# Two transformer layers on one core: the output bias of attention in four tiles, a count moved, the last routing amid expert tiles, other banks at a stage's exit, the last rows in two stores

## The chip, the core and the metric

The kernel runs on one core of one Trainium2 chip. A core has engines with a queue of instructions each: TensorE (PE in the profile; PEld its weight loads), VectorE (DVE), ScalarE (ACT), GpSimd (POOL) and SyncE (SP), which here only issues DMAs. [...] They wait for each other through semaphores. Matmuls write into PSUM[...]; everything else is in SBUF or in DRAM. The metric is the device time of one execution in microseconds.

## The reference

Eight sequences of 512 rows and 512 columns pass through two layers. All weights and activations are float32.

```python
# layer 0
x = layernorm(x + attn0(x))     # causal, 16 heads of 32; q, k, v and output with a bias
#   attn0: out = softmax(mask(q k^T / sqrt(32))) v ;  return out @ WO.T + WO_b
x = layernorm(x + moe(x))       # router: softmax over 8 experts, the two largest, weights renormalised
#   expert: (silu(gate) * up) @ down, with low-rank additions; y = sum of the two experts by weight
# layer 1
x = layernorm(x + attn1(x))     # norm, 8 query heads on 2 key heads of 64, no mask, own residual
x = layernorm(x + ffn(x))       # hidden 1408, weights integers minus 128 by a scale per row
```

The kernel sends each row only to its two experts, by a table of rows that it builds on the way.

## The kernel before, in words

**Attention of layer 0** (`attention0`, lines 1298 to 1653). The loop goes over sequences b = 0..7, groups of four heads g = 0..3 and units u = 0..2 of the causal score matrix (UNITS, key tiles 0; 1 and 3; 2). A unit is: scores on TensorE (L65), the exponential on ScalarE (L1476), one or two `affine_select` on POOL that zero what lies above the diagonal (L1486; two in unit 1), and one unit later the product with v (L1503) and VectorE's sums of p (L1511). At unit 1 the group before is normalised: row sums rs (L1518), their reciprocal (L1521) and the product into aoT (L1522). Between these stand pieces of other work that `plan(b)` hands out: q, k and v of the groups to come, the output projection of sequence b-1 (`project`, L1402, with layernorm, L190 to L198, and stores into `rows`), and its routing. For sequences 0 to 5 the normalised rows are turned through DRAM: 32x32 blocks on VectorE (L98), four stores and one load (L103, L106), then the router's logits (`score`, L504) at unit 2 of group 3. Sequence 6 is turned on TensorE (L1427), sequence 7 after the heads. `choose` finds the two experts (L523 to L554), `dispatch` the ranks (L568 to L578), `one_hot` (L591, L592) and `enter` (L601 to L603) put rows into the table.

**The order.** TensorE's order is the order in which the program is written (`in_order`). VectorE, ScalarE, POOL and SP in attention 0 get theirs from a planner at build time: by its own costs it sees what is ready, and takes the earliest in the program of that. From the expert stage (step 12) to the end of attention 1 all are in program order; in the feed-forward part the planner orders again, up to the last rows.

**Buffers that the change meets.** The pool "mm" has two PSUM banks; each `mm(...)` takes the one that was taken the time before last, and waits until it has been read. Scores have one buffer of four banks. SBUF tiles with the same tag share a buffer: `first_turned` (tag "row", L1575 on) takes that of `row`, which holds the bias of v and the output bias; `first_rows` takes that of a sequence's x. `first_turned` receives, at unit 1 of group 3 of sequence 7, the first expert rows turned (L924, copied by ScalarE at L925).

**The output bias** is added to x by one POOL instruction for a sequence, at group 2 (L1595). In the trace the planner has put it where x has just landed, in group 3 of the sequence before (for sequences 2 to 7).

**The first expert tiles** (`Tiles`) begin amid the end of attention 0. They use rows of sequences 0 to 5 only, after a count that says whether four tiles of each of the first four experts are full (`soon`, L613 to L615). A `step` on TensorE is one half of the hidden layer for a pair of tiles (`half`, 16 matmuls, L958) and one `down` (4 matmuls, L983); it also fetches rows (POOL, L873) and turns them. The routing of sequence 7 stands between steps 3 to 6.

**Exit of attention 1** (`batches`, from L1955). The last projections use four banks; residuals (L1804), statistics and norms (L1823) follow on VectorE. `IntegerFfn.run` then opens its PSUM pools, `p_gu` first. **End**: `last_rows` normalises a tile of 128 rows at a time; the last on VectorE (L1288), then one store by ScalarE's queue (L1293).

## Time and profile before

| what | value |
|---|---|
| median of 3 runs | 2107.35 us (2106.85 to 2108.73) |
| profiled execution | 2106.08 us |
| its span, first to last instruction | 2104.2 us |
| attention 0, to about 690 us | TensorE busy 677.4 us |
| routing amid tiles, 690 to 770 us | TensorE busy 78.1 of 80 us |
| expert tiles, 770 to 1062 us | TensorE busy 291.5 of 292 us |
| attention 1, 1062 to 1600 us | TensorE busy 535.9 of 538 us |
| feed-forward, 1600 to the end | TensorE busy 491.6 us |

The times are those of one profiled execution, which differs from the median by 1.3 us. In a row of the time line the first number is the start in us from the span's start, the second the length; "xN" is how many instructions of one kind were merged; the bracket at the end tells how long the engine was idle before and which instruction ended that ("<-"). In a row of waits the three numbers are the sum in us, the count and the longest.

### The profile page before, as it was taken

The page shows a single profiled execution, that of the slowest core. Times are in us where ns is not written, and L with a number is a line of the kernel's source. Part 1 is how long each engine was busy: PE and PEld are TensorE (multiplying, and loading weights), DVE is VectorE, ACT ScalarE, POOL GpSimd, SP SyncE. Part 2 cuts the span into 40 slices and gives each one's busy share as a digit, 9 for nine tenths or more (in the row PEclk, how much of TensorE's full clock was granted, in tenths as well). Part 3 has the DMA queues.
Part 4 walks back from the last instruction along what each step waited for, and adds up shares of the span by engine and source line. Part 5 has one row for each costly group of instructions (what it writes and reads, how often), then busy time and mean ns, then how long its engine had stood idle before and what let it go on. Part 6 is the DMA issues. An engine that isn't in the chain of part 4 may idle for free. (4 is left out here: it accounts for less than half of the span.)

```text
span 2104.2 us, 35813 instructions
## 1 busy us (share of the span) xinstructions
PE 2074.4 (99%) x15074; PEld 1048.8 (50%) x15074; DVE 1270.6 (60%) x1963; ACT 606.8 (29%) x840; POOL 496.0 (24%) x488
## 2 busy tenths in 40 slices
PE   8999999999999999999999999999999999999998
PEld 2333333333334677774433333333335888888886
DVE  2666776776768623234257898887867644555443
ACT  2333433324333111111143333333332322222222
POOL 2343534434333221222042221223101000000000
PEclk9999999999999999999999999999999999999999
DMA  9020303415222568877451322132102311111000
GB/s 326 22 65 38 101 22 110 136 52 156 85 98 102 172 199 239 251 227 209 149 206 51 100 81 71 56 95 81 41 1 71 100 41 61 60 61 60 21 21 22
DMA packets 181946, 213.39 MB, mean 101 GB/s; under 512 B 72570, under 2 KB 125818, under 8 KB 178706
## 3 DMA queue, kind: packets, MB, share of 16 engines
q1 hardware_dynamic: 170496, 175.34, 26.8%
q0 software_dynamic: 10560, 34.61, 5.6%
q8 instruction: 121, 1.98, 0.4%
q10 hardware_dynamic: 722, 1.07, 0.1%
q14 instruction: 47, 0.39, 0.1%
HBM read 132.58 MB, written 78.40 MB: 100 GB/s over the span
## 5 line engine op out<-in xcount | busy, mean ns | idle before, releaser
L1077 POOL TENSOR_TENSOR g_total<-g_total,r_inv 128x512 f32<-128x512 f32 x64 | 90.1, 1408 | 488.3 <-DVE r_inv L1862 269.9
L1476 ACT ACTIVATE p<-sc 128x2048 f32<-128x2048 f32 (+1 forms) x96 | 153.0, 1594 | 174.7 <-PE sc L65 150.7
L1511 DVE TENSOR_TENSOR p<-p 128x1536 f32<-128x1536 f32 (+2 forms) x96 | 149.5, 1557 | 77.6 <-POOL p L1486 74.4
L1227 DVE SCALAR_TENSOR_TENSOR hT<-ps_u,vec,sg 128x512 f32<-128x512 f32 x88 | 65.6, 745 | 187.2 <-PE ps_u L1222 187.1
L1238 PE MATMUL ps_f<-ffn_w,h_half 128*128 128x512 f32 x664 | 168.1, 393 | 2.6 <-DVE h_half L1233 2.0
L958 PE MATMUL ps_gu<-xrT,experts 128*128 128x256 f32 x736 | 166.7, 380 | 0.4 <-DMA xrT<-pair 0.4
L958 PEld LDWEIGHTS ps_gu<-xrT,experts 128*128 128x128 f32 x736 | 139.5, 190 | 35.6 <-issue 19.2
L1832 ACT ACTIVATE p<-sc 128x1024 f32<-128x1024 f32 x128 | 124.2, 1022 | 100.2 <-PE sc L65 91.5
L1862 DVE RECIPROCAL r_inv<-r_inv 128x512 f32<-128x512 f32 x32 | 107.1, 3346 | 67.8 <-ACT r_inv L1074 67.8
L1238 PEld LDWEIGHTS ps_f<-ffn_w,h_half 128*128 128x128 f32 x664 | 122.9, 188 | 34.6 <-DVE h_half L1233 8.0
L1222 PE MATMUL ps_g<-x_high,ffn_w 128*128 128x512 f32 x352 | 137.3, 390 | 0.9 <-DVE x L1804 0.9
L1222 PE MATMUL ps_g<-x_low,ffn_w 128*128 128x512 f32 x352 | 137.2, 390 | 0.0
L1222 PE MATMUL ps_u<-x_low,ffn_w 128*128 128x512 f32 x352 | 137.1, 390 | 0.0
L1222 PE MATMUL ps_u<-x_high,ffn_w 128*128 128x512 f32 x352 | 137.1, 389 | 0.0
L65 PE MATMUL sc<-qT,kT 64*64 64x512 f32 x1024 | 124.7, 602 | 1.2 <-ACT qT L1729 0.9
L65 PE MATMUL ps_q<-experts 128*32 128x512 f32 x1024 | 120.8, 601 | 4.9 <-DMA experts<-in_xT 4.6
L65 PE MATMUL ps_v<-experts 128*32 128x512 f32 x1024 | 120.9, 595 | 0.0
L1851 PE MATMUL av<-p,v 128*64 128x512 f32 x512 | 120.9, 594 | 0.0
L1486 POOL TENSOR_SCALAR_AFFINE_SELECT p<-p 128x512 f32<-128x512 f32 x128 | 82.7, 657 | 157.6 <-ACT p L1476 155.0
L1225 ACT ACTIVATE sg<-ps_g,vec 128x512 f32<-128x512 f32 x88 | 60.6, 689 | 199.8 <-PE ps_g L1222 199.8
L65 PE MATMUL ps_o<-attn_out,aoT 128*64 128x512 f32 x512 | 116.4, 598 | 0.0
L65 PE MATMUL ps_k<-experts 128*32 128x512 f32 x1024 | 116.3, 595 | 0.0
(278 smaller groups left out, 3248.3 us busy)
## 6 DMA issues: line engine op xcount, KB each, us to landing
results<-y SPq DMA_DIRECT2D x68, 256.0 KB, 3.2
pair<-xrT SPq DMA_DIRECT2D x30, 512.0 KB, 3.0
xrT<-pair SPq DMA_DIRECT2D x120, 128.0 KB, 3.8
turned<-turned SPq DMA_DIRECT2D x56, 256.0 KB, 4.0
x<-in_x SPq DMA_DIRECT2D x8, 1024.0 KB, 8.6
rows<-x SPq DMA_DIRECT2D x32, 256.0 KB, 2.3
x<-rows SPq DMA_DIRECT2D x16, 512.0 KB, 12.5
experts<-in_xT SPq DMA_DIRECT2D x7, 1024.0 KB, 8.5
```

The source lines that it names most:

```text
L65: nc.tensor.matmul(out[m], lhsT=lhsT[:, m], rhs=rhs, start=start, stop=stop)
L958: nc.tensor.matmul(ps[:, j, :], lhsT=w, rhs=xT[:, c, :], start=c == 0, stop=c == ND - 1)
L1077: self.nc.gpsimd.tensor_tensor(self.total, self.total, r_inv, ALU.add)
L1222: nc.tensor.matmul(ps, lhsT=w[:, ts(dc, P)], rhs=x[:, dc, :], start=(dc, i) == (0, 0), stop=(dc, i) == (ND - 1, 1))
L1227: nc.vector.scalar_tensor_tensor(hT, u, vec[:, V_SU + c : V_SU + c + 1], sg, ALU.mult, ALU.mult)
L1238: self.nc.tensor.matmul(os[t], lhsT=h[:, ts(t, P)], rhs=self.weights(2 * NHID + c), start=(c, i) == (0, 0), stop=(c, i) == (NHID - 1, 1))
L1476: nc.scalar.activation(p, sc[:, :, :width], AF.Exp, scale=scale)
L1486: nc.gpsimd.affine_select(out=first, in_=first, pattern=[[0, 4], [1, P]], compare_op=ALU.is_ge, fill=0.0, base=0, channel_multiplier=-1)
L1511: nc.vector.tensor_tensor(total[:, :, P * kt :], total[:, :, P * kt :], p[:, :, at : at + w], ALU.add)
L1832: nc.scalar.activation(p, sc, AF.Exp, scale=scale)
L1851: nc.tensor.matmul(st["av"][HD * j : HD * (j + 1), :], lhsT=st["v"][:, kt, HD * j : HD * (j + 1)], rhs=p[:, j, :], start=kt == 0, stop=kt ...
L1862: nc.vector.reciprocal(r_inv, r_inv)
```

## The change

1. **Output bias.** For sequences 1 to 7 the bias is added in four POOL instructions of 128x512, tile g at unit 1 of group g, each ordered behind the last select of that unit. For sequence 0 it stays one instruction, at unit 1 of group 2.
2. **Count and table.** `soon` no longer counts on TensorE; it copies four columns of the running count. The count is taken later, in `tables`, beside the one that is there. In sequence 7 the read of the table's bank is ordered ahead of the product into aoT of the group before (`behind`). A small tile (`lane`) moves into a buffer that exists.
3. **Routing of sequence 7.** `choose` and `dispatch` go inside steps 4 and 5, between the half and the down, instead of ahead of steps 4 and 5; the one_hots go ahead of steps 6 and 7, and `enter` behind step 7.
4. **Exit of attention 1.** The pool `p_o` is opened ahead of `p_gu`, so they exchange banks, and the projections take the second bank of a scores buffer instead of the first.
5. **Last rows.** The last tile is normalised in two halves of 256 columns, each stored by its own DMA, on SP's and on ScalarE's queue.

```diff
@@ Router.enter, soon, tables
-        nc.vector.tensor_tensor(self.table, ps, self.table, ALU.add)
+        read = nc.vector.tensor_tensor(self.table, ps, self.table, ALU.add)
         nc.vector.tensor_tensor(self.table, held, self.table, ALU.add)
+        return read
...
-    def soon(self, pool, ps, held):
+    def soon(self, pool):
         nc, half = self.nc, E // 2
-        nc.tensor.matmul(ps, lhsT=self.ones, rhs=self.carry, start=True, stop=True)
-        nc.vector.tensor_reduce(held, ps[:, :half], AX.X, ALU.min)
-        nc.vector.tensor_scalar(held, held, float(SOON * P), None, ALU.is_ge)
+        self.soon_carry = pool.tile([P, half], F32, name="r_soon_carry")
+        nc.vector.tensor_copy(self.soon_carry, self.carry[:, :half])
...
+        half = E // 2
+        ps, soon = ps[:, :E], ps[:, E:]
         nc.tensor.matmul(ps, lhsT=self.ones, rhs=self.carry, start=True, stop=True)
+        nc.tensor.matmul(soon, lhsT=self.ones, rhs=self.soon_carry, start=True, stop=True)
+        nc.vector.tensor_reduce(held_soon, soon, AX.X, ALU.min)
+        nc.vector.tensor_scalar(held_soon, held_soon, float(SOON * P), None, ALU.is_ge)
@@ Tiles.step
-    def step(self):
+    def step(self, amid=lambda: None):
...
+        amid()
         if i:
             self.down(i)
@@ IntegerFfn.run
+            self.p_o = phase.enter_context(tc.tile_pool(name="d_o", bufs=1, space=PSUM, reuse_waits="tile"))
             self.p_gu = phase.enter_context(tc.tile_pool(name="d_gu", bufs=2, space=PSUM, reuse_waits="tile"))
-            self.p_o = phase.enter_context(tc.tile_pool(name="d_o", bufs=1, space=PSUM, reuse_waits="tile"))
@@ last_rows
         if t == NT - 1:
-            nc.vector.tensor_scalar(x, x, mv[:, 0:1], rstd, ALU.subtract, ALU.mult)
+            for i, queue in enumerate((nc.sync, nc.scalar)):
+                half = x[:, ts(i, D // 2)]
+                nc.vector.tensor_scalar(half, half, mv[:, 0:1], rstd, ALU.subtract, ALU.mult)
+                queue.dma_start(out=env.ins.out[b][ts(t, P), ts(i, D // 2)], in_=half)
@@ attention0: scores, behind, plan, the loop, its end
+            if u == 1 and b:
+                x = xs[b][:, g, :]
+                with tc.issue_after(select.ins):
+                    nc.gpsimd.tensor_tensor(x, x, row[:, 1, :], ALU.add)
+            elif (g, u) == (2, 1):
+                with tc.issue_after(select.ins):
+                    nc.gpsimd.tensor_tensor(xs[b], xs[b], row[:, 1:2, :].to_broadcast([P, NT, D]), ALU.add)
...
+        def behind(first, second):
+            tc.add_manual_dep(second.ins, first.ins.name,
+                              mybir.DependencyInfo(mybir.DependencyClass.NoSync, mybir.DependencyReason.DATA),
+                              reason="reads of a bank that is wanted")
...
-                todo[1, 2].append(lambda: enter(one_hot(b - 2, range(NT))))
+                if last:
+                    todo[1, 2].append(lambda: behind(enter(one_hot(b - 2, range(NT))), normed[0]))
+                else:
+                    todo[1, 2].append(lambda: enter(one_hot(b - 2, range(NT))))
...
-                    nc.gpsimd.tensor_tensor(xs[b], xs[b], row[:, 1:2, :].to_broadcast([P, NT, D]), ALU.add)
...
-        choose(b, P)
-        tiles.step()
-        dispatch(b, tiles.bank, P)
+        tiles.step(lambda: choose(b, P))
+        tiles.step(lambda: dispatch(b, tiles.bank, P))
@@ Attention1.batches
-        banks += [p_sc.tile([P, 2, S], F32, tag="sc", name="ps_o1")[:, 0, :] for _ in range(2)]
+        banks += [p_sc.tile([P, 2, S], F32, tag="sc", name="ps_o1")[:, 1, :] for _ in range(2)]
```

More of the change, by code (lines that the diff above doesn't have):

```diff
@@ L471, in __init__ @@
         nc.gpsimd.iota(i, pattern=[[0, 1]], base=0, channel_multiplier=1)
-        lane = pool.tile([P, 1], F32, name="r_lane")
+        room = tmp.tile([P, S], F32, tag="r_inv", name="r_columns_i", bufs=2)
+        lane = room[:, E * E_TILES : E * E_TILES + 1]
         nc.vector.tensor_copy(lane, i)
@@ L476, in __init__ @@
             nc.vector.tensor_scalar(self.signed[:, t : t + 1], lane, float(P * t - GAP + (P * t >= GAP)), None, ALU.add)
-        i = tmp.tile([P, S], F32, tag="r_inv", name="r_columns_i", bufs=2)[:, : E * E_TILES].bitcast(I32)
+        i = room[:, : E * E_TILES].bitcast(I32)
         nc.gpsimd.iota(i, pattern=[[1, E * E_TILES]], base=0, channel_multiplier=0)
@@ L627, in fixed, with tables @@
         return lambda e, j: tokens[:, e, j : j + 1]
-    def tables(self, pool, ps, held):
+    def tables(self, pool, ps, held_soon, held):
         nc = self.nc
@@ L1292, in last_rows @@
             nc.scalar.activation(x, x, AF.Identity, bias=shift, scale=rstd)
-        nc.scalar.dma_start(out=env.ins.out[b][ts(t, P), :], in_=x)
+            nc.scalar.dma_start(out=env.ins.out[b][ts(t, P), :], in_=x)
 def attention0(env, guard, keep, routes, experts, dram, p_mm, tiles_ctx):
@@ L1458, in enter @@
         def enter(rows, mm=mm, columns=HD):
-            router.enter(mm([P, E * E_TILES], "ps_table"), *rows, columns)
+            return router.enter(mm([P, E * E_TILES], "ps_table"), *rows, columns)
         def scores(b, g, u):
@@ L1485, in scores @@
                 first = p[:, :, at : at + P]
-                nc.gpsimd.affine_select(out=first, in_=first, pattern=[[0, 4], [1, P]], compare_op=ALU.is_ge, fill=0.0,
-                                        base=0, channel_multiplier=-1)
+                select = nc.gpsimd.affine_select(out=first, in_=first, pattern=[[0, 4], [1, P]], compare_op=ALU.is_ge,
+                                                 fill=0.0, base=0, channel_multiplier=-1)
                 at += S - P * kt
+            if u == 1 and b:
[5 more added lines that the diff above has]
+                    nc.gpsimd.tensor_tensor(xs[b], xs[b], row[:, 1:2, :].to_broadcast([P, NT, D]), ALU.add)
             for thunk in merging.pop(n, []):
@@ L1521, in normalise @@
             nc.vector.reciprocal(r_inv, r_inv)
-            nc.vector.tensor_tensor(aoTs[b][:, g, :], av, r_inv, ALU.mult)
+            normed[0] = nc.vector.tensor_tensor(aoTs[b][:, g, :], av, r_inv, ALU.mult)
             guard.watch_inverses(r_inv)
-        merging = {}
+        merging, normed = {}, [None]
+        def behind(first, second):
+            tc.add_manual_dep(second.ins, first.ins.name,
+                              mybir.DependencyInfo(mybir.DependencyClass.NoSync, mybir.DependencyReason.DATA),
+                              reason="reads of a bank that is wanted")
         def plan(b):
@@ L1579, in soon @@
         def soon():
-            tiles.of_soon = router.soon(routes, mm([P, E], "ps_count"), guard.routed[:, 0:1])
+            tiles.of_soon = router.soon(routes)
         begun = phase.enter_context(ExitStack())
@@ L1652, in attention0 @@
         order.close()
-    return router, tiles, router.tables(routes, p_mm.tile([P, E], F32, tag="mm", name="ps_count"), guard.routed[:, 1:2])
+    return router, tiles, router.tables(routes, p_mm.tile([P, E + E // 2], F32, tag="mm", name="ps_count"), *(guard.routed[:, i : i + 1] for i in range(2)))
 class Attention1:
```

## The prediction

> **What bounds the kernel now.** I read the page's first part, then the list of waits of TensorE (who waited for whom), then the time line around each wait, engine by engine.

> ```profile
> PE 2074.4 (99%) x15074; PEld 1048.8 (50%) x15074; DVE 1270.6 (60%) x1963; ACT 606.8 (29%) x840; POOL 496.0 (24%) x488
> ```

> TensorE is busy for 2074.4 of 2104.2 us. Of the 29.8 us left, 9.0 lie behind its last matmul and 4.6 ahead of its first. No edit removes more than one small matmul, so only TensorE's idle stretches can be won, and any other engine counts only where it makes TensorE wait. The waits that the change touches:

> ```profile
> PE av L1503 <- POOL p L1486: 1.9, 3, 1.0
> PE ps_logits L504 <- DMA x1T<-turned: 1.8, 2, 1.5
> PE ps_x1T L1427 <- DVE g_routed L614: 1.5, 1, 1.5
> PE ps_g L1222 <- DVE x L1804: 0.9, 1, 0.9
> PE ps_r L65 <- ACT logits L1440: 0.8, 1, 0.8
> PE ps_rank L65 <- DVE earlier L553: 0.7, 1, 0.7
> PE rs L1518 <- ACT first_turned L925: 0.6, 1, 0.6
> ```

> Columns: total us, count, longest. Lines one and three to six are what the change can win: 5.8 us, plus something at the end. Lines two and seven are where I expect it to lose.

> **Part 1, the output bias.** Before, one POOL instruction of 4.56 us per sequence (L1595) stood in POOL's order between the selects of the sequence before it, and waited there for x to land:

> ```profile
> 583.68 4.57 POOL L1595 TENSOR_TENSOR x<-x,row 128x2048 f32<-128x2048 f32 x1 [1.56 <-DMA x<-in_x]
> 588.19 1.23 POOL L1486 TENSOR_SCALAR_AFFINE_SELECT p<-p 128x512 f32<-128x512 f32 x2
> ```

> The selects behind it come late and TensorE waits 0.27, 0.60 and 1.01 us at 164, 503 and 588. With the adds behind the selects these waits go: **-1.9**. Sequence 0 keeps a whole add of 4.56 us, now at 48 instead of 21; there the next select is needed at 55, so it costs nothing; a cover smaller by 2 us would begin to cost.

> The new adds are 128x512. The nearest rows are the adds into the experts' weights (1.27 us alone) and into g_total (1.41 to 1.6 beside VectorE); I take 1.3. In most groups the next select comes over 5 us later, so the add is hidden. Two places are not free.

> (a) *Group 2 of sequences 1 to 6.* The select pair of unit 1 runs just as VectorE normalises the previous sequence; its four transposes, four stores to DRAM, the read back (8.3 us) and the router's logits on TensorE hang on these norms one after the other. The add falls on norms 3 and 4:

> ```profile
> 395.07 1.41 POOL L1486 TENSOR_SCALAR_AFFINE_SELECT p<-p 128x512 f32<-128x512 f32 x2
> 395.14 2.53 DVE L195 TENSOR_SCALAR x<-x,mv,rstd 128x512 f32<-128x512 f32 x4 [1.48 <-POOL rstd L193]
> ...
> 644.34 2.78 DVE L195 TENSOR_SCALAR x<-x,mv,rstd 128x512 f32<-128x512 f32 x4
> ...
> 706.17 1.92 DVE L195 TENSOR_SCALAR x<-x,mv,rstd 128x512 f32<-128x512 f32 x4 [1.18 <-POOL rstd L193]
> ```

> Four norms take 1.92 us when POOL is quiet and 2.78 beside the g_total add of 644.51 (1.41 us): 0.86 late. In the trace the read back landed before TensorE reached the logits by 1.61, 0.52, 1.16 and 0.73 us (at 247, 331, 501, 586), and later than that at 162 and 416 (waits of 0.30 and 1.46). A start needs 0.14 after the landing. With all of it 0.86 later the waits grow by 0.86 (162), 0 (247), 0.48 (331), 0.86 (416), 0 (501) and 0.27 (586): **+2.5**. [...] Queued behind the norms on SP are the stores of rows, the next load of x and the read back; all move together.

> (b) *Group 3 of sequence 7.* The tile first_turned takes the one buffer of row (tag "row"), and now the last reader of row is the add of this group. Before, row was last read at 588:

> ```profile
> 670.06 1.07 ACT L925 COPY first_turned<-ps_xrT 128x512 f32<-128x512 f32 x2
> 670.23 1.26 POOL L1486 TENSOR_SCALAR_AFFINE_SELECT p<-p 128x512 f32<-128x512 f32 x2 [2.60 <-DVE r_hots L535]
> 670.69 1.07 PE L1518 MATMUL rs<-p,ones 128*32 128x512 f32 x8 [0.57 <-ACT first_turned L925]
> ```

> The add comes behind the pair of selects: 671.49 + 1.3 = 672.8. Only then may ScalarE copy; the first copy ends at 673.4, which frees one of the two "mm" banks that the row sums (rs) need. TensorE goes on at 673.5 instead of 670.7: **+2.8**. Behind the copies on ScalarE stand the reading of rs and the next exponential; on TensorE the next scores. Ends: 0 if the planner's order avoids it, 3.3 if VectorE's add at 672.03 slows the bias add.

> At unit 1 of group 1 the add meets the one_hot instructions of VectorE (0.3 us each, 16 of them); 1.2 us late, they still end before their matmuls (slack 1 us or more at 375.9 and 386.8, one sequence to the next). I take 0; 0.1 in each of five sequences if the slack is used up.

> **Part 2, the count and the table.** Two matmuls leave the heads (0.32 from ps_count to the next start) and the bank ps_count with them; the first transposes of sequence 6 then take the bank of k, free since 644.6, and the second ones the table's bank, whose read goes ahead of the 0.68 us product L1522. Read at 648.4, TensorE would reach the scores at 649.1, when ScalarE's exponential (ends 648.8 then) has freed their banks, instead of 650.12: -1.0. VectorE's copies of x1T still stand behind its adds until 651.2 (1.59 us L1511), so query(7, 3) starts near 651.95 instead of 652.62. I take **-0.8**; ends -1.3 and -0.3. The count comes back in tables(): its row L640 there costs 0.14 from start to start; **+0.15** for the second matmul. Two VectorE operations of 0.15 are in a stage with VectorE a third busy: 0.

> **Part 3, routing of sequence 7 amid tiles.** The logits' copy is now covered by the 3.62 us of a half tile: -0.76. Between choose and dispatch lie 5.5 us of TensorE before and after, but ScalarE loads the exponential's table later: behind the silu of that half tile, whereas before it loaded while waiting:

> ```profile
> 723.54 1.28 ACT L525 ACT_TABLE_LOAD   x1
> 725.12 0.23 ACT L525 ACTIVATE tmp<-tmp 128x32 f32<-128x32 f32 x1 [0.30 <-DVE tmp L524]
> ```

> ps_r at 727.2, silu to 727.0, table to 728.3, exponential to 728.6, then the same 20 operations, 3.95 us, to 732.5, with a y copy of 0.69 among them 733.2. TensorE asks at 732.7: a wait of 0 to 1.2, taken as 0.5 instead of 0.72. Sum **-1.0**. [...] The table of sequence 7 is entered one step later, the gathers of the fixed tiles with it; they landed 4.7 us after issue, and their VectorE transposes come two steps later: 0, or +-0.4 at the DMA wait of 758.

> **Part 4, exit of layer 1.** ps_g no longer waits 0.85 for the last residual. But the next stop hardly moves: VectorE's own order decides it.

> ```profile
> 1613.58 1.22 DVE L1137 TENSOR_SCALAR ffn_w<-ffn_i 128x2048 fp32r<-128x2048 int32 x1
> 1614.71 0.75 DVE L1227 SCALAR_TENSOR_TENSOR hT<-ps_u,vec,sg 128x512 f32<-128x512 f32 x1
> ...
> 1616.21 1.16 PE L1238 MATMUL ps_f<-ffn_w,h_half 128*128 128x512 f32 x4 [0.62 <-issue]
> ```

> hT stands behind norms and a conversion that don't depend on ps_g, and TensorE stands idle for 0.62 at ps_f already; 0.85 earlier, it idles 1.47. Only if the planner moves hT forward is it won. **-0.3**, ends 0 and -1.4.

> **Part 5, two stores.** The last norm (0.55) ends at 2099.37, the store is issued to 2099.74 and landed near 2103.2. Two norms of some 0.3 end at about 2099.45; the first half is stored 0.2 earlier, the second has half the bytes. No row shows a 128 KB store to the output; **-0.3**, ends +0.1 and -0.6.

> **Sum.** -1.9 + 2.5 + 2.8 - 0.8 + 0.15 - 1.0 - 0.3 - 0.3 = +1.15. On the profiled execution: 2106.08 to 2107.2, of which 1.9 lie outside the span. The median of the runs is 2107.35, so **2108.5 us**.

> **Rivals.** *Every turned sequence is late* (slower). The DMA slack above is that of one execution. If the reads back come when TensorE is ready, the full 0.86 is paid in all six sequences: 5.2 instead of 2.5; with (b) at 3.3 and the one_hots at 0.5 the sum is +4.9, 2112.2. It decides from a mean loss of 0.9 per sequence. For it: two of six waited already. Against: four had 0.5 to 1.6 to spare.

> [...]

> *The bias is not the gain it seems* (no change). The adds leave, but the selects stay late behind the adds into the experts' weights (2.27 us beside VectorE): -1.9 falls away, and (a) with it, since POOL's order is then another: about +0.5, 2107.9.

> **How the numbers follow.** The runs spread by 0.09%; 0.2% (4.2 us, 2103.1 to 2111.6) is about what a measurement can tell from no change. The sum as worked out 0.47, its own range 2106 to 2111.5 from the ends of (a), (b) and part 3, with 0.04 beyond 2111.6; late sequences 0.31, of which 0.29 above; no new waits 0.15, of which 0.13 below; no gain 0.07. Faster 0.13, same 0.54, slower 0.33. The range that leaves out 2 in 10, half of each far case: 2103.5 to 2113.

> **What would show it.** Right: no waits of av on POOL; norms of 3.2 to 3.5 us for four in sequences 1 to 6, and ps_logits waiting in four of them; rs of 7, 3 behind first_turned for over 3 us; ps_x1T waiting under 0.7; ps_r not waiting, ps_rank still; ps_f at 1616 waiting longer. Wrong: first_turned copied straight after the exponential, norms of 2.5 us, or an order of VectorE or ScalarE that has changed elsewhere in layer 0.

## The result, and the profile after

The kernel after takes 2113.03 us in the median of 13 runs (2109.55 to 2117.22), beside 2107.58 (2105.61 to 2111.23) for the kernel before: a ratio of 1.0026, 95% interval 1.0017 to 1.0035. Measured again in another series it is 1.0023 (1.0014 to 1.0032). It is 4.2 to 5.5 us slower, where I had forecast 1.15. The profiled execution takes 2110.86 us, with a span of 2108.8: 4.6 us more than the one before.

The page's line of busy times, of the kernel after:

```profile
PE 2075.9 (98%) x15074; PEld 1048.4 (50%) x15074; DVE 1288.2 (61%) x1965; ACT 607.9 (29%) x840; POOL 505.6 (24%) x509
```

TensorE stands idle for 32.9 us instead of 29.8 (span less busy time). Its list of waits (sum in us, count, longest):

```profile
PE sc L65 <- ACT qT L1751: 3.6, 2, 2.8
PE rs L1535 <- ACT first_turned L931: 3.3, 1, 3.3
...
PE ps_rank L65 <- DVE earlier L554: 1.6, 1, 1.6
...
PE ps_logits L505 <- DMA x1T<-turned: 1.1, 3, 0.6
...
PE ps_f L1245 <- PE ps_u L1229: 0.8, 1, 0.8
PE ps_x1T L1437 <- DVE r_table L603: 0.7, 1, 0.7
...
PE ps_rank L65 <- DVE both L550: 0.6, 1, 0.6
```

The waits of av on POOL, of ps_g and of ps_r are gone, and ps_x1T waits half as long. In their place stand rs with 3.3 instead of 0.6, the ranks with 1.6 + 0.6 instead of 0.7, and a new one, 2.8 us for qT where attention 1 begins.

The stop at rs, by the time lines of POOL, ScalarE and TensorE:

```profile
670.42 1.26 POOL L1502 TENSOR_TENSOR x<-x,row 128x512 f32<-128x512 f32 x1
...
671.72 1.08 ACT L931 COPY first_turned<-ps_xrT 128x512 f32<-128x512 f32 x2 [2.59 <-POOL x L1502]
...
672.36 1.06 PE L1535 MATMUL rs<-p,ones 128*32 128x512 f32 x8 [3.28 <-ACT first_turned L931]
```

The copy waits for the add, and TensorE for the copy. The norms of the sequence before, and what POOL does beside them:

```profile
396.86 1.41 POOL L1496 TENSOR_SCALAR_AFFINE_SELECT p<-p 128x512 f32<-128x512 f32 x2
398.24 1.45 POOL L1502 TENSOR_TENSOR x<-x,row 128x512 f32<-128x512 f32 x1
...
396.92 3.50 DVE L195 TENSOR_SCALAR x<-x,mv,rstd 128x512 f32<-128x512 f32 x4 [1.48 <-POOL rstd L193]
```

Four norms take 3.50 us instead of 2.53. One by one they take 0.85, 0.85, 1.50 and 0.53: the third, which takes 0.53 without the add, loses 0.97 to it, and so in each of sequences 1 to 6.

Side by side on their start times, TensorE runs 2.1 us later than before at the end of the experts, another 3.6 later 50 us into attention 1, and 1.2 sooner again at the exit of layer 1. These three numbers set the questions: the losses of layer 0, whether the 3.6 us belong to the change, and a gain that is four times what I had written.

### The profile page after: what moved, and what is told of

It reads as the page before. It is cut to its first block, busy times and chain, and to the rows that moved or that the text cites. A ratio compares the mean times of both kernels' runs of the same rounds, so it can differ in the third digit from the quotient of the medians.

```text
span 2108.8 us, 35839 instructions
## 1 busy us (share of the span) xinstructions
PE 2075.9 (98%) x15074; PEld 1048.4 (50%) x15074; DVE 1288.2 (61%) x1965; ACT 607.9 (29%) x840; POOL 505.6 (24%) x509
## 5 line engine op out<-in xcount | busy, mean ns | idle before, releaser
L1486 ACT ACTIVATE p<-sc 128x2048 f32<-128x2048 f32 (+1 forms) x96 | 153.1, 1594 | 175.9 <-PE sc L65 152.3
L65 PE MATMUL sc<-qT,kT 64*64 64x512 f32 x1024 | 125.2, 604 | 4.0 <-ACT qT L1751 3.6
L65 PE MATMUL ps_q<-experts 128*32 128x512 f32 x1024 | 121.3, 603 | 4.8 <-DMA experts<-in_xT 4.5
L65 PE MATMUL ps_v<-experts 128*32 128x512 f32 x1024 | 120.9, 594 | 0.0
L65 PE MATMUL ps_o<-attn_out,aoT 128*64 128x512 f32 x512 | 116.4, 598 | 0.0
L65 PE MATMUL ps_k<-experts 128*32 128x512 f32 x1024 | 116.3, 594 | 0.0
```

Source lines behind the costliest of these rows:

```text
L65: nc.tensor.matmul(out[m], lhsT=lhsT[:, m], rhs=rhs, start=start, stop=stop)
L1486: nc.scalar.activation(p, sc[:, :, :width], AF.Exp, scale=scale)
```

## The experiments

My theory after the two traces: the time goes to the stop at the shared buffer, to the add of group 2 and to the routing; what attention 1 lost is an event of that execution. The rival: the change brings the stop in attention 1 about. Times below are medians; each series measured the kernel before beside its kernels, and differences are to that.

**Both kernels again.** No edit.

> The kernel before, once more, for its mean clock in each execution and for a second trace. Theory A (the 4 us lost where attention 1 begins, and the half clock after it, are an event that some executions have and others not, in both kernels): the ratio is 1.000 within 0.0005, most executions show a mean clock of 0.999, one or two 0.998 or less and those are 2 us longer or more per 0.001. Theory B (the change brings the stop at the beginning of attention 1 about): every execution shows 0.999 and the spread is under 3 us.

> The kernel after, once more, for a second trace. Both theories: ratio 1.0026, some 2113 us, mean clocks of 0.995 to 0.999. Theory A: the stop of 2.76 us ahead of the second sequence's scores in attention 1 is not there in every trace; if it is absent here, the span is near 2105 to 2107 plus 1.7 us for each stretch of half clock. Theory B: it is there again, at the same instruction, with 2 us or more.

Before: ratio 1.0001 (0.9992 to 1.0009), mean clocks 0.998 and 0.999 alone, which is also all that 151 executions of the kernel before show. After: 1.0023, mean clocks from 0.996 to 0.999. In the second trace of the kernel after, no stop stands ahead of the second sequence's scores in attention 1, so it is not the change's, and theory B falls on that point. But the clock had an answer of its own. Windows of the time line of the kernel after, second trace; columns are the stretch, its length, busy us of TensorE, its weight loads, VectorE, ScalarE and POOL, then the granted clock of TensorE, and DMA:

```profile
668.00:672.00 4.00, 0.81 (x8) 0.16 (x8) 3.82 (x7) 1.08 (x2) 2.49 (x3) 1.00 0.00 0
672.00:675.50 3.50, 3.50 (x25) 2.15 (x22) 3.40 (x3) 2.61 (x4) 0.63 (x1) 0.51 0.02 5
675.50:679.00 3.50, 3.50 (x17) 3.07 (x17) 2.85 (x3) 0.98 (x2) 2.05 (x1) 1.00 0.00 0
733.00:737.00 4.00, 1.95 (x10) 1.30 (x8) 3.79 (x20) 0.00 (x0) 0.00 (x0) 0.99 0.40 101
737.00:740.40 3.40, 3.29 (x6) 1.74 (x7) 2.77 (x21) 0.00 (x0) 0.00 (x0) 0.51 0.00 0
740.40:744.00 3.60, 3.60 (x18) 2.97 (x17) 2.42 (x12) 1.87 (x2) 0.00 (x0) 1.00 0.34 104
```

Behind each of the two new stops, at rs and at the ranks, the clock is at half for 3.4 us. In the first trace of the same kernel neither stop did this; there the stop in attention 1 did (half clock from 1083.81 for 3.41 us). Executions of the kernel after with a mean clock of 0.999 take 2109.7 us in the first series and 2108.9 in the second, those at 0.996 take 2115.7 and 2112.7. So the spread of the kernel after, which is wider than that of the kernel before, goes with the clock.

**The last add one unit sooner, and part 3 undone.** Each alone on the kernel after, then both.

```diff
-            if u == 1 and b:
+            if b and u == (0 if (b, g) == (NB - 1, 3) else 1):
```
```diff
-        tiles.step(lambda: choose(b, P))
-        tiles.step(lambda: dispatch(b, tiles.bank, P))
+        choose(b, P)
+        tiles.step()
+        dispatch(b, tiles.bank, P)
```

> The kernel after with one placement changed: for sequence 7 the add of group 3 stands behind the select of unit 0 instead of unit 1, so that the buffer of row is free before first_turned is copied. Theory A (the shared buffer costs 2.7 us at this place, and the long stop there is one of those that bring the half clock): rs at 669 waits under 0.8 us instead of 3.28, the time falls by 2.7 us at least and by up to 4.5, to 2108.5 to 2110.3, and the mean clock is 0.998 or more in most executions. Rival (the buffer only hides another late thing, ScalarE's exponential or the bank): rs still waits over 2 us and the time falls by under 1 us.

> The kernel after with part 3 undone: choose and dispatch ahead of steps 4 and 5 as before. Theory A (part 3 lost 0.7 us: it removed the wait of 0.76 for the logits and made the one for the ranks 2.17 instead of 0.72): ps_r waits 0.8 again, ps_rank 0.7, the time falls by 0.7 us, to about 2112.3; that is inside what five rounds can tell, so the waits decide. Rival (part 3 gained its 1.0 us and the longer wait for the ranks is of one execution): the waits ahead of routing sum to 1.0 us more than in the kernel after.

> The kernel after with both of the earlier edits: the last add one unit sooner and part 3 undone. Theory A (the loss is these two stops, each with a half clock that follows in some executions): no stop of TensorE over 1.5 us in layer 0 that is not a DMA's, mean clock 0.998 to 0.999 as in the kernel before, 2105.0 to 2106.0 us, ratio 0.9990 to 0.9995. Rival (half of what the two edits gave is drift, or the stretches of half clock come from elsewhere): 2107 us or more, and clocks of 0.997 remain.

The add alone: 0.9998 (0.9990 to 1.0006), 4.2 us below the kernel after of the same series. Its rows:

```profile
670.05 1.07 ACT L931 COPY first_turned<-ps_xrT 128x512 f32<-128x512 f32 x2
...
670.68 1.07 PE L1535 MATMUL rs<-p,ones 128*32 128x512 f32 x8 [0.57 <-ACT first_turned L931]
```

The copy follows the exponential at once and rs waits 0.57 us, as in the kernel before; the rival falls. Part 3 undone alone: 1.0011 (1.0004 to 1.0017), 1.3 us below the kernel after, ps_r waiting 0.76 and ps_rank 0.72 as before. Both: 0.9996 (0.9987 to 1.0004), no clock under 0.998. Both edits together win about what theory A said, and end only 1 us ahead of the kernel before.

**The add of group 2 behind unit 2**, on top of both edits, and alone on the kernel after.

```diff
-            if u == 1 and b:
+            if b and u == (2 if g == 2 else 1):
...
-            elif (g, u) == (2, 1):
+            elif not b and (g, u) == (2, 1):
```

> The kernel with both edits, and the add of group 2 moved from unit 1 to unit 2 in sequences 1 to 7, away from the norms of the sequence before. Theory (the add costs each four norms 0.8 us and with them the read back of the turned rows): four norms take 2.5 us again instead of 3.4, the logits wait 0.9 us in sum (the mean of two traces of the kernel before) instead of 2.2 (the mean of the four traces with the add there), the time falls by 1.3 us to 2104 to 2104.7. Rival (what moves the read back is the DMA queues from execution to execution, not the norms): norms of 2.5 us, logits still waiting 1 to 3 us in sum, the time unchanged within 0.5 us.

> The kernel after with one edit: the add of group 2 behind the select of unit 2. The shared buffer and part 3 stay as they are. Theory (the edit gives the same 4 us here as on top of the other two, since it acts on sequences 1 to 6 and they on sequence 7): ratio 0.0020 below that of the kernel after, about 1.0004 (the kernel after had 1.0026 and 1.0023); third norms of 0.53 us; rs at 669 still waits 3.3 us, the ranks 2.2 us, clocks of 0.997 remain. Rival (the 4 us need the other edits, or were the chance of those runs): a gain under 2 us, ratio 1.0014 or more.

On top of both: 0.9976 (0.9967 to 0.9985), 2100.59 us: 4.2 us below the kernel with both edits, three times what I expected. The logits no longer wait at all. The kernel with both edits, and then the one with group 2's add later, around the third select of a group (rows of VectorE, POOL and TensorE):

```profile
141.33 3.50 DVE L195 TENSOR_SCALAR x<-x,mv,rstd 128x512 f32<-128x512 f32 x4 [1.49 <-POOL rstd L193]
...
148.80 3.34 DVE L1538 RECIPROCAL r_inv<-r_inv 128x512 f32<-128x512 f32 x1
...
152.21 1.60 POOL L1084 TENSOR_TENSOR g_total<-g_total,r_inv 128x512 f32<-128x512 f32 x1 [8.12 <-DVE r_inv L1538]
153.77 0.63 POOL L1496 TENSOR_SCALAR_AFFINE_SELECT p<-p 128x512 f32<-128x512 f32 x1
...
150.78 3.64 PE L65 MATMUL ps_q<-experts 128*32 128x512 f32 x32
154.46 0.64 PE L1520 MATMUL av<-p,v 128*32 128x256 f32 x8
```

```profile
141.20 2.54 DVE L195 TENSOR_SCALAR x<-x,mv,rstd 128x512 f32<-128x512 f32 x4 [1.49 <-POOL rstd L193]
...
147.70 3.34 DVE L1538 RECIPROCAL r_inv<-r_inv 128x512 f32<-128x512 f32 x1
...
151.12 1.61 POOL L1084 TENSOR_TENSOR g_total<-g_total,r_inv 128x512 f32<-128x512 f32 x1 [8.58 <-DVE r_inv L1538]
152.69 0.63 POOL L1496 TENSOR_SCALAR_AFFINE_SELECT p<-p 128x512 f32<-128x512 f32 x1
...
150.66 3.64 PE L65 MATMUL ps_q<-experts 128*32 128x512 f32 x32
154.11 0.61 PE L1520 MATMUL av<-p,v 128*32 128x256 f32 x8
```

The norms take 0.96 us longer with the add beside them, and the reciprocal (L1538), which stands behind them on VectorE, starts 7.47 us after their start instead of 6.50. From there the delay goes on to the add into g_total on POOL and so to the select, which is 1.1 us later. From ps_q to av it is 3.68 us instead of 3.45. Start by start, the two traces part by 0.19 to 0.22 us at this av in each of sequences 1 to 6, 1.2 us in all, and the brackets show 0.04 or less of each: the modelled end of ps_q covers the wait. The logits' waits are the other part: 1.6 us in the mean of eleven traces with the add in unit 1 (0.5 to 3.4), none in this one. Together that is 2.8 of the 4.2 us; where the rest arises is open.

Alone on the kernel after, the edit gives 1.0008 (1.0000 to 1.0016), 2 to 4 us below it by the means and ratios of the two series. The stops at rs and at the ranks remain, and with them mean clocks of 0.996 in 8 of 14 executions. Those 8 take 2109.3 us in the mean, the 3 at 0.999 take 2104.6: executions of one kernel lie 4.7 us apart with their clock.

**The exit of layer 1 alone** (part 4), on the kernel before.

```diff
+            self.p_o = phase.enter_context(tc.tile_pool(name="d_o", bufs=1, space=PSUM, reuse_waits="tile"))
             self.p_gu = phase.enter_context(tc.tile_pool(name="d_gu", bufs=2, space=PSUM, reuse_waits="tile"))
-            self.p_o = phase.enter_context(tc.tile_pool(name="d_o", bufs=1, space=PSUM, reuse_waits="tile"))
...
-        banks += [p_sc.tile([P, 2, S], F32, tag="sc", name="ps_o1")[:, 0, :] for _ in range(2)]
+        banks += [p_sc.tile([P, 2, S], F32, tag="sc", name="ps_o1")[:, 1, :] for _ in range(2)]
```

> The kernel before with part 4 alone (the pools exchanged, the second bank of the scores buffer). Theory (the planner, once ps_g need not wait, puts hT ahead of the conversion of the weights and of two norms): the waits of 0.85 for ps_g and 0.6 for ps_f become one of about 0.8, everything behind runs 1.2 us sooner, ratio 0.9994. Rival (the gain of 1.17 us seen in the kernel after was a shift that came from the stop ahead of it, and the prediction's 0.3 holds): 0.3 us, ratio 0.9999, ps_f waits 1.4.

It takes 2104.58 us, 1.24 below the kernel before, with a ratio of 0.9997 (0.9988 to 1.0005), so the total alone doesn't tell it from nothing. The time line of VectorE does:

```profile
1610.56 0.75 DVE L1227 SCALAR_TENSOR_TENSOR hT<-ps_u,vec,sg 128x512 f32<-128x512 f32 x1 [0.23 <-issue]
1611.23 0.17 DVE L1813 BATCH_NORM_AGGREGATE mv<-stats 128x2 f32<-128x6 f32 x1
1612.88 0.55 DVE L1823 TENSOR_SCALAR x<-x,mv,rstd 128x512 f32<-128x512 f32 x1 [1.47 <-POOL rstd L1817]
1613.34 1.22 DVE L1137 TENSOR_SCALAR ffn_w<-ffn_i 128x2048 fp32r<-128x2048 int32 x1
```

hT stands ahead of the norms and of the conversion, where before it came behind them at 1614.71. ps_g doesn't wait, ps_f waits 0.8. From the twentieth matmul ahead of ps_g to the fortieth behind the first ps_f it is 22.1 us in each of the fourteen traces with part 4, and 23.0 in each of the four without: 0.9 us are won here.

**The stop filled.** On the kernel with part 3 undone, matmuls whose product nobody reads go ahead of rs, first six, then three. The output is untouched; TensorE only has work while it waits.

```diff
             total, av = acc
+            if (b, g) == (NB - 1, 2):
+                fill = p_sc.tile([P, 4, S], F32, tag="sc", name="fill")
+                for j in range(3):
+                    nc.tensor.matmul(fill[:, j, :], lhsT=env.ident, rhs=total[:, j, :], start=True, stop=True)
```

> The kernel after with part 3 undone and with six matmuls of 128x512 whose product nobody reads put ahead of the row sums rs at 669, so that TensorE works through most of the stop that the shared buffer makes there. The stop itself stays. Theory A (a stop of 3.3 us makes the granted clock fall to half for 3.4 us in more than half of the executions, which costs up to 1.7 us beyond the stop): rs goes on at the same time, the clock is 1.0 behind it in the trace, mean clocks rise from 0.998 and 0.997 to 0.999 and 0.998, and the time is 1.0 to 1.5 us below that with part 3 undone alone (2109.9), 2108.4 to 2108.9. Rival (the fall of the clock is not due to the stop, or the matmuls only draw it elsewhere): clocks and time as with part 3 undone alone, or 0.5 us above.

> The kernel after with part 3 undone and three instead of six matmuls ahead of the row sums at 669. Six took 5.42 us (0.90 each) and so went 2.2 us beyond the stop that they were to fill; three take 2.7 us and end inside it. Theory A (the stop brings the half clock): rs waits 0.6 us or less behind the three and starts when it did without them, no half clock behind it, mean clock over the runs 0.9986 or more as with six (0.9987), against 0.9978 without; the time falls by the clock's share, 0.9 in 1000 or less: 1.0 to 1.9 us below part 3 undone alone, a ratio of 1.0002 to 1.0006 against 1.0011. Rival (the clock is not what costs the time): clock 0.9986 or more and the ratio still 1.0011.

> The kernel after with part 3 undone, once more, beside the two that follow: the stop of 3.3 us at rs is there and open. Theory A (the stop costs 2.7 us as a wait beyond the 0.57 of the kernel before, and about 1.3 us on the mean by the half clock that it brings): mean time 3.5 to 4.3 us above that of the kernel without the stop, mean clock 0.998 or less, executions at 0.997 some 3 us above those at 0.999. Rival (the half clock moves the mean clock but not the end, since the engines behind TensorE wait anyway): 2.7 us above it, and no slope of time on clock.

> The same kernel with the stop filled by three matmuls that nobody reads, once more. Theory A: 2.7 us above the kernel without the stop and 1.0 to 1.6 us below the one with the open stop, mean clock 0.9987 or more. Rival: the same time as with the open stop within 0.5 us. The runs before gave a difference of 0.7 us with an uncertainty of as much, on two calls.

> The same kernel with the last add one unit sooner, so that there is no stop, as the lower end for the two above. Both theories: 1.0 to 1.3 us below the kernel before, mean clock 0.9986 to 0.9989.

Six were too many: they take 5.42 us, 2.2 beyond the stop, and the ratio is 1.0019 (1.0010 to 1.0029), so the expected time was missed. Three fit:

```profile
668.07 2.84 PE L1536 MATMUL fill<-p,ident 128*128 128x512 f32 x6
671.25 1.06 PE L1539 MATMUL rs<-p,ones 128*32 128x512 f32 x8 [0.34 <-ACT first_turned L931]
```

From the last transpose (ps_xrT) to rs it is 3.55 us with the open and with the filled stop, and 0.85 without one. What comes then, from rs to the logits of sequence 7, is the same work in all of them:

| trace | ps_xrT to rs | rs to logits | half clock behind rs |
|---|---|---|---|
| no stop, both edits (two traces) | 0.85 | 51.00, 51.00 | none |
| filled by three (two traces) | 3.55 | 51.00, 51.00 | none |
| after, first and second trace | 3.55 | 51.00, 52.57 | none, 3.41 us |
| open stop, part 3 undone (two traces) | 3.55 | 52.58, 53.95 | 3.41, 6.83 us |
| after with group 2 later | 3.55 | 53.57 | 6.83 us |

The filled stop kept the clock in all three traces, the open one lost it in four of six (the sixth is part 1 alone, below: 51.00, none). Mean clocks rose from 0.9978 (33 executions) to 0.9988 (34, those with six matmuls among them). The totals say less. Side by side, the open stop gives 1.0012 (1.0003 to 1.0020), the filled one 1.0011 (1.0002 to 1.0020), no stop 0.9991 (0.9982 to 1.0000); by the means of the executions, in two series, filling gave 0.7 and 0.8 us, each with a standard error of 0.6 to 0.8, where the six traces give 1.4 us on the mean. That the stop brings the half clock, and that this stretches the work behind it by 1.6 to 2.9 us when it comes, is shown. How much filling this one stop gives on the mean stays open between nothing and 1.7 us.

**Part 1 alone, and parts 2 and 5 alone**, on the kernel before, with the lines of the diff above.

> The kernel before with part 1 alone, as in the kernel after. Theory (part 1 wins back its waits of av on POOL, 1.9 to 2.8 us, and loses 3.5 to 4.2 by the add of group 2, 2.7 by the shared buffer and 0.5 to 1.5 by the half clock that follows): 4.0 to 6.0 us slower than before, ratio 1.0019 to 1.0028, no av waiting on POOL, third norms of 1.5 us, rs waiting 3.3. Rival (part 1 by itself is neutral, as my sum had it with +3.4, because half of the loss comes from part 3 and the rest): under 3.4 us, ratio 1.0016 or less.

> The kernel before with parts 2 and 5 alone (the count and the table; the last rows in two stores). Theory, from the traces of the kernels with all parts: part 2 gives 0.85 us at 646 to 659 and costs about 0.15 in the tables, part 5 gives nothing (the time behind the last matmul is 8.95 us without it and 9.0 to 9.2 with it): 0.7 us below the kernel before, ratio 0.9996 to 0.9997. Rival (the prediction's terms: 0.8, 0.15 and 0.3): 0.95 us; the tail tells the two apart, 9.0 us or more against 8.65.

Part 1: 1.0026 (1.0016 to 1.0037), 6.1 us slower, as much as the whole change; the other parts together come to about nothing. Parts 2 and 5: 0.9996 (0.9987 to 1.0005), 0.5 us below in the median, 0.8 in the mean, with ps_x1T waiting 0.75 instead of 1.5; behind the last matmul lie 9.06 us, so part 5 gives nothing. In this trace ps_g doesn't wait either (why is open), but hT still comes behind the conversion, at 1615.50, and ps_f waits 1.54: without hT moved forward, nothing is won at the exit.

**Choose amid a tile, dispatch later**, on the kernel with the three placements mended and part 3 otherwise undone.

```diff
-        choose(b, P)
+        tiles.step(lambda: choose(b, P))
         tiles.step()
         dispatch(b, tiles.bank, P)
```

> The kernel with the three edits (last add sooner, group 2's add later, part 3 undone), and of part 3 only choose amid step 4; dispatch ahead of step 6, behind the down of step 5, so one down (1.9 us) later than in the kernel after. Theory (VectorE's chain from choose to the ranks is 2.2 us late in the kernel after because a copy of y, a product h and two transposes of rows stand among its twenty instructions): ps_r does not wait, the ranks wait 0.3 us instead of 2.2, time 1.0 to 1.4 us below the kernel with the three edits (2100.6): 2099.4, ratio 0.9971. Rival (whatever stands behind choose waits for the exponential's table, so the later place only moves the wait): ranks wait 1 us or more, time 2100.5 to 2101.

It takes 2100.11 us, a ratio of 0.9971 (0.9960 to 0.9982): the lowest median here, 5.6 us below the kernel before. ps_r doesn't wait, and the ranks wait 0.72 and not 0.3. From the logits to attention 1 it is 340.6 us instead of 341.4, so 0.8 us was won and not 1.0 to 1.4; the interval of the totals overlaps that of the kernel without this edit.

## Why the prediction was wrong

Three steps failed. The clock had no term; it makes 2.3 to 3.3 us of the median. The delay of the norms was followed to the logits and not to the reciprocal behind them, +1.2. Part 3 was put at -1.0 and came to about +1.0. Part 4 won 0.6 more than its term, against these.

**Part 1, waits of av: -1.9.** Right in kind, a little small. They sum to 1.9 to 4.0 us in four traces with the whole add (mean 2.8), and to 0.2 at most in those with quarter adds: about -2.6.

**(a), +2.5: place right, one consequence missed.** The norms lost 0.97, not 0.86; the logits waited 1.6 us on the mean, against 0.5 on the mean of four traces with the whole add, so that this term was +1.1: the one trace I had read, with 1.8, is not the usual one. But I followed only what hangs on the norms by data. The failing step is "Queued behind the norms on SP are the stores of rows ...": behind them on VectorE stands the next reciprocal, and through POOL the next select. That is another +1.2. The two make +2.3, near the +2.5 by chance. Moving the add gave 2 to 4 us by the totals, since the logits then don't wait either. Of the four norms only the third loses time to the add: it starts 0.23 us behind the add and ends 0.28 behind its end, in all six sequences. The ends of (a) in the forecast's range are shown by no run; the runs showed 0.97 us lost at the norms of each of these sequences and the two delays that come from it.

**(b), +2.8.** Right to 0.1 us (2.70), and the copy's waiting for the add as described. What I had no term for is the clock behind the stop: in four of the six traces with the stop of 3.3 us open it was at half for 3.41 or 6.83 us behind it, and the work from rs to the logits took 1.6 to 2.9 us longer. I had the stop's length beside me and counted the wait alone.

**Part 2, -0.8 + 0.15.** Right: 0.86 in the traces between 590 and 659 us.

**Part 3, -1.0: wrong in sign.** The -0.76 came; the ranks wait 2.17 instead of 0.72. The step that failed is "the same 20 operations, 3.95 us, to 732.5, with a y copy of 0.69 among them". VectorE, in the kernel after:

```profile
734.45 0.19 DVE L550 TENSOR_TENSOR both<-r_hots 128x32 f32<-128x32 f32 x1
734.56 0.68 DVE L966 TENSOR_TENSOR h<-ps_gu,h 128x512 f32<-128x512 f32 x1
735.16 0.15 DVE L554 TENSOR_TENSOR earlier<-earlier,both 128x8 f32<-128x8 f32 x1
735.24 0.70 DVE L910 STREAM_TRANSPOSE xrT<-xr 128x512 f32<-128x512 f32 x1
735.86 0.12 DVE L554 TENSOR_TENSOR earlier<-earlier,both 128x8 f32<-128x8 f32 x1
735.91 0.70 DVE L910 STREAM_TRANSPOSE xrT<-xr 128x512 f32<-128x512 f32 x1
736.53 0.12 DVE L554 TENSOR_TENSOR earlier<-earlier,both 128x8 f32<-128x8 f32 x1
```

The half tile that now stands ahead of dispatch brings its product h and two transposes of rows, 2.08 us, among the four small additions that the ranks wait for. Moving a step past a queue meant counting what the queue gets in between. The load of the exponential's table took 1.28 us in this trace, and the next ACTIVATE began 0.02 us behind it. From the logits to attention 1 it is 342.4 us without a half clock in the kernel after, and 341.2 to 342.3 (median 341.4) in thirteen traces with the old order: about +1.0 instead of -1.0, and 1.5 to 1.8 more where the clock fell at the ranks, in three of four traces (without another wait of 0.9 us that one of them has).

**Part 4, -0.3: nearer its far end**, -0.9 at the exit: the planner moved hT forward. I had named the condition and chosen the other side. (The first pair of traces shows -1.2, of which 0.3 is the trace of the kernel before.)

**Part 5, -0.3: nothing.** The two norms take 0.73 us instead of 0.55, and the time behind the last matmul is 9.0 us as before.

Put together without the clock: -2.6 + 2.3 + 2.7 - 0.9 + 1.0 - 0.9 = +1.6; executions of the kernel after whose clock stayed at 0.999 are some 2.0 us above the median of the kernel before in either series. Part 1 alone agrees: its terms make +2.4, and its two executions at 0.999 are 2.6 and 3.3 us above. The rest, 2.3 to 3.3 us of the median, goes with the clock. The rival that named 2112.2 comes near the number by luck: it needed 5.2 us from (a), which came to 2.3, and 0.5 from the one_hots, for which TensorE never waited, and it had no term for the clock.

## What to carry over

Follow a delay down the queue of the engine that is late, and not only along the data: the 1 us that the norms lost cost as much again through the reciprocal behind them (1.2 us beside the logits' 1.1). When a step is moved past other work, count what that work puts into each queue in between. A stop of TensorE can cost more than its length: behind the one of 3.3 us the clock was at half in four of six traces, and the work there took 1.6 to 2.9 us longer. So shorten it first. Filling it with work kept the clock in three traces of three; a gain in the total isn't shown.

## What the hardware showed beyond that

```profile
667.38:670.79 3.41, 1.70 (x16) 0.85 (x8) 3.13 (x16) 1.75 (x1) 1.59 (x3) 1.00 0.04 11
670.79:674.21 3.42, 1.85 (x25) 0.63 (x26) 3.25 (x5) 1.77 (x5) 0.89 (x1) 1.00 0.00 0
```

```profile
669.61:673.02 3.41, 0.15 (x4) 0.15 (x8) 3.20 (x8) 0.81 (x3) 2.50 (x3) 1.00 0.00 0
673.02:676.43 3.41, 3.41 (x26) 0.94 (x21) 2.91 (x3) 1.43 (x4) 0.00 (x0) 0.50 0.02 5
```

In the first the stop falls across the border of two steps, TensorE works 1.7 us or more in each, and the clock stays; in the second it falls into one step, and the clock is at half in the next. Over the 18 traces, up to TensorE's last matmul, the half clock followed all 7 full-clock steps with less than 1.5 us of work, 1 of 16 with 1.5 to 2.0, and none of some 10,960 with more. These steps were not all idle: in the one ahead of the half clock at 1083.81 TensorE worked 1.29 us. In the two traces above the stop of 3.3 us kept or lost the clock by where it fell. This is read from eight half clocks, and what else they hang on isn't shown.

What stopped the first trace of the kernel after in attention 1 is open: ScalarE's copy of qT began 3.8 us after the last matmul it waits for, while the DMA engines were busy all the time (share 1.0), as they are in traces without the stop. Four other traces, all of the last series and one of them with parts 2 and 5 alone, show a stop of 1.4 us at the same place, and thirteen traces none; it wasn't tested.
